# A fused attention and feed-forward block: first loads in chunks, put-off rotations, bank reads ahead of the maximum tree, and early row statistics

## The chip, the cores and the metric

The kernel runs on one core of a Trainium2 chip. The metric is the device time of one execution in microseconds. TensorE (PE) multiplies matrices and writes to PSUM banks; VectorE (DVE), ScalarE (ACT) and GpSimd (POOL) do the elementwise work; SyncE (SP) and ACT issue the transfers (DMA). Each engine works through its own list of instructions in order, and a semaphore holds an instruction back until what it needs is there.

## The reference

Two batches of 512 rows by 1024, all in fp32, and a context of 1024 rows by 1024 for each batch. `x` is the running row matrix:

```python
x = x + quantized_matmul(layernorm(x), ctx)             # both sides rounded to 0..255
x = x + ffn0(layernorm(x))                              # W.T, bias, LoRA mixed by a softmax router
h = layernorm(x)
q = rope(h @ wq)            # 32 heads of 128
k, v = rope(ctx @ wk), ctx @ wv                         # 8 heads, each for 4 query heads
x = x + softmax(q @ k.T / sqrt(128) + mask) @ v @ wo
x = x + ffn1(layernorm(x))                              # W_up.T, LoRA of the top-1 expert
```

## The kernel before

PE's order is written out by hand in the whole program. DVE, ACT and POOL follow the order of a scheduler, except in the attention, where the order of the code is taken as it stands. SP's list holds most transfers.

**Products in sevens.** Big products are done by a scheme with seven instead of eight products of quarter matrices. `left_sums` and `right_sums` make the four sums of quarters on each side. `seven` (for keys, values and queries) and `seven_onto` (for the output projection and the two feed-forward layers) run the products in a set order: 1, 2, 6, 7, 5, 4, 3 or 1, 6, 2, 7, 5, 4, 3. Product 2 is added in PSUM onto the bank of product 1, 4 onto that of 7, 3 onto that of 5; so before product 4 may start, someone must have read product 7 out of the bank they share. In `seven_onto` product 1 is copied out by ACT (L267), product 6 is added by DVE in L269, and all others by DVE in L272; POOL adds a further term in L274. The products of fp32 matrices appear in the trace as records of four to a product of 256 contraction rows and eight to one of 512.

**Banks.** PSUM has a pool "b" of four banks (products, attention results, the broadcast maxima) and a pool "wide" of two double banks (scores, transposes).

**The stages.** First come the keys and values of batch 0 in the order keys, values, keys, values (two quads each), with the quantized product of both batches woven in as `side` work; then batch 1, the first feed-forward layer (`linear`, `routed`), the queries in eight quads (`queries`), the attention, and the second feed-forward layer. Keys and queries are rotated by `rope`: two ACT operations of half the partitions (L192, L193), and three on DVE (L194, L197, L198); the result is then stored to DRAM from SP's queue.

**The attention loop** (`attention`) is a pipeline over 64 heads. A step `n` has three phases: the scores of head n+2 (L686, with the mask added on DVE in L700); then three or four products of the output projection of an earlier group (`stretches`) or, in the first steps, the last products of the last quad of queries (`extra["products"]`), alternating with the four operations of the maximum `tree` (L708, L710, L712, L714); then the third phase:

```python
            if old:
                old.turn_sum()
                old.attend(0)
            if mid:
                mid.place_maximum()
                mid.exponential(0)
```

`turn_sum` and `turn_maximum` transpose on PE (L650), reduce on DVE (L652) and store a row of 512 numbers to DRAM from ACT's queue (L659); `from_row` reads such a row back on all partitions, also from ACT's queue (L665). `place_maximum` copies the row of maxima to a bank (ACT, L728); `exponential` adds it (DVE, L732), takes the exponential (ACT, L735) and sums on POOL (L738 to L743). `attend` multiplies with the values (L749), and ACT copies the result out (L757). POOL normalizes in L760. A cycle of four steps holds 4, 3, 4 and 3 stretches.

**The tail.** When the last step with new scores is over, `normed` makes the normalized, transposed rows of batch 0 for the second feed-forward layer: for each of the four row tiles statistics (L163, L165), a root on ACT (L167), a reciprocal (L168), the scaling (L170) and eight transposes (L185), woven with the last steps of the attention. Then come the gate (L874) and `linear`.

Of the kernel before, what the change touches and what calls it, by code (L numbers as in the profile page):

```python
# [18 lines left out]
P = 128  # L19
# [20 lines left out]
def decoder_kernel(  # L40
# [119 lines left out]
    def layernorm(x_t):  # L160
        stats = small([P, 2, 6])
        for i in range(2):
            nc.vector.bn_stats(stats[:, i, :], x_t[:, ts(i, HALF)])  # L163
        mv = small([P, 2])
        nc.vector.bn_aggr(mv, stats)  # L165
        rstd = small([P, 1])
        nc.scalar.activation(rstd, mv[:, 1:2], AF.Sqrt, bias=eps_t)  # L167
        nc.vector.reciprocal(rstd, rstd)  # L168
        h = u4([P, D])
        nc.vector.tensor_scalar(h, x_t, mv[:, 0:1], rstd, ALU.subtract, ALU.mult)  # L170
        return h
# [32 lines left out]
    def left_sums(eng, a11, a12, a21, a22, fresh):  # L204

        s3, s2, s4 = fresh(), fresh(), fresh()
        eng.tensor_tensor(s3, a11, a21, ALU.subtract)
        eng.tensor_tensor(a21, a21, a22, ALU.add)
        eng.tensor_tensor(s2, a21, a11, ALU.subtract)
        eng.tensor_tensor(s4, a12, s2, ALU.subtract)  # L210
        return [a11, a12, s4, a22, a21, s2, s3]

    def right_sums(eng, b11, b12, b21, b22, fresh):

        t3, t2, t4 = fresh(), fresh(), fresh()
        eng.tensor_tensor(t3, b22, b12, ALU.subtract)
        eng.tensor_tensor(b12, b12, b11, ALU.subtract)
        eng.tensor_tensor(t2, b22, b12, ALU.subtract)
        eng.tensor_tensor(t4, b21, t2, ALU.subtract)
        return [b11, b21, b22, t4, b12, t2, t3]  # L220
# [193 lines left out]
    def keys(b, q, ctx_ops, w):  # L414
# [15 lines left out]
        return pair(group(0), group(1))  # L430

    def values(b, q, ctx_ops, w):
# [24 lines left out]
        return pair(blocks(0), blocks(1))  # L457

    def transposed_norm(b, places):

        h = None
        for t in range(NT + 1):
            ahead = layernorm(rows(b, t)) if t < NT else None
# [5 lines left out]
    def normed(b, tile, n):  # L469
# [4 lines left out]
        else:  # L474
# [3 lines left out]
            [[quarters[t // 2][j][:, :, ts(t % 2, P)] for t in range(NT)] for j in range(2)],  # L478
        )
# [116 lines left out]
    def queries(q, h_ops, w):  # L596
        def head(m):
# [7 lines left out]
            def emit(i, j, src):  # L605
                dst = u2([P, HALF]) if (i, j) == (0, 0) else src
                rope(dst, src, 0, ATT_SCALE)
                nc.sync.dma_start(q_d[j][4 * q + 2 * i + m], dst)

# [164 lines left out]
    def attention(extra):  # L774
# [23 lines left out]
        for n in range(-2, total + GRP + 1):  # L798
# [9 lines left out]
            if n == 2:  # L808
                w_ops = {i: output_operand(0, i) for i in (1, 6, 2, 7, 5, 4, 3)}
# [23 lines left out]
            for _ in range(3 + k % 2):  # L833
                next(tree, None)
                next(stretches, None)
# [3 lines left out]
            for _ in range(extra.pop(n, 0)):  # L839
                next(tree, None)  # L840
                next(extra["products"])
# [3 lines left out]

            if old:
                old.turn_sum()
                old.attend(0)
            if mid:
                mid.place_maximum()  # L850
# [9 lines left out]
            if old:  # L860
                old.attend(1)
            yield
# [51 lines left out]
    wk_raw, ctx_raw = [], [None] * 4  # L914
    for i, (wh, ch, kh) in enumerate((((0, 0), 0, 0), ((0, 1), 1, 0), ((1, 1), 0, 1), ((1, 0), 1, 1))):
        w = u4([P, 4, 256])
        (nc.sync if i % 2 else nc.scalar).dma_start(w, wk[0, wh[0], wh[1]])
        t = u8([P, 4, HALF])
        src = ctxT_in[0, ts(ch, 4 * P), ts(kh, HALF)].rearrange("(c p) n -> p c n", p=P)
        nc.scalar.dma_start(t[:, 0:2, :], src[:, 0:2, :])  # L920
        nc.sync.dma_start(t[:, 2:4, :], src[:, 2:4, :])
        wk_raw.append(w)
        ctx_raw[2 * ch + kh] = t
    wk_raw[2:] = wk_raw[3], wk_raw[2]
    late = u4([P, 2, HALF])
    nc.sync.dma_start(cos_t[0], cos_in[:, 0:HALF])
    nc.sync.dma_start(sin_t[0], sin_in[:, 0:HALF])
    nc.sync.dma_start(late[:, 0, :], cos_in[:, HALF:S2])
# [203 lines left out]
```

## Time and profile before

| | us |
|---|---|
| median of 4 runs | 2553.16 (2551.92 to 2556.35) |
| profiled execution | 2552.19 |
| its span | 2550.3 |
| PE busy | 2454.4 (96%) |
| DVE busy | 1867.0 (73%) |
| POOL busy | 1010.3 (40%) |
| ACT busy | 531.1 (21%) |
| DVE idle ahead of L732, behind ACT's L728 | 67.6 |
| DVE idle ahead of L272, behind PE | 126.5 |

The mean granted clock of PE is 0.991. In the page a group of instructions is given by line, engine, operation and tiles; "idle before, releaser" is the time in which that engine stood still just ahead of such an instruction, and what ended most of it. A busy PE is not PE at its peak: at the reduced clock the same matmul shows a longer time. The steady part of the attention runs from about 1141 to 2327 us, the tail with the last layer from there to 2550.

### The profile page before, as it was taken

The page shows a single profiled execution, that of the slowest core. Times are in us where ns is not written, and L with a number is a line of the kernel's source. Part 1 is how long each engine was busy: PE and PEld are TensorE (multiplying, and loading weights), DVE is VectorE, ACT ScalarE, POOL GpSimd, SP SyncE. Part 2 cuts the span into 40 slices and gives each one's busy share as a digit, 9 for nine tenths or more (in the row PEclk, how much of TensorE's full clock was granted, in tenths as well). Part 3 has the DMA queues.
Part 4 walks back from the last instruction along what each step waited for, and adds up shares of the span by engine and source line. Part 5 has one row for each costly group of instructions (what it writes and reads, how often), then busy time and mean ns, then how long its engine had stood idle before and what let it go on. Part 6 is the DMA issues. An engine that isn't in the chain of part 4 may idle for free.

```text
span 2550.3 us, 19683 instructions
## 1 busy us (share of the span) xinstructions
PE 2454.4 (96%) x6849; PEld 1213.9 (48%) x6856; DVE 1867.0 (73%) x2039; ACT 531.1 (21%) x618; POOL 1010.3 (40%) x536
## 2 busy tenths in 40 slices
PE   7999999999999998899999999999999999997999
PEld 3747567554444443344444444444444444443553
DVE  6778736447776557788888888888888888887542
ACT  1211112101222212222222222222222222223000
POOL 0000100210000002276767666766777676766221
PEclk9999999999999999999999999999999999999899
DMA  7334322024883312423322332443233323333200
GB/s 251 126 124 146 123 92 95 13 84 160 309 313 111 104 67 60 137 56 109 109 68 84 111 106 69 119 144 91 77 93 112 87 74 99 112 80 86 83 34 33
DMA packets 146946, 277.53 MB, mean 109 GB/s; under 512 B 29152, under 2 KB 46576, under 8 KB 145824
## 3 DMA queue, kind: packets, MB, share of 16 engines
q1 hardware_dynamic: 106064, 234.39, 27.7%
q10 hardware_dynamic: 40352, 41.17, 6.7%
q8 instruction: 55, 0.90, 0.2%
q0 software_dynamic: 432, 0.71, 0.1%
q14 instruction: 43, 0.35, 0.1%
HBM read 217.24 MB, written 58.98 MB: 108 GB/s over the span
## 4 chain that ended last, share of the span: by engine, by line
PE 45%; DVE 14%; issue 7%; ACT 1%; DMA 1%; POOL 0%; ACTq 0%; POOLq 0%; DVEq 0%; SPq 0%
PE b L299 18%; PE wide L686 14%; PE b L749 11%; DVE u L708 4%; DVE u L732 3%; DVE u L272 2%; PE wide L650 2%; DVE small L652 1%; DVE u L700 1%; DVE u L712 1%; PE b L874 1%; DVE u L714 1%; DMA row<-small 1%; ACT b L728 0%; DVE u L269 0%
## 5 line engine op out<-in xcount | busy, mean ns | idle before, releaser
L299 PE MATMUL b<-u,u 128*128 128x512 f32 (+1 forms) x3648 | 1421.8, 546 | 41.7 <-DVE u L272 16.8
L299 PEld LDWEIGHTS b<-u,u 128*128 128x128 f32 x3648 | 690.6, 191 | 736.2 <-issue 628.8
L686 PE MATMUL wide<-u,u 128*128 128x512 f32 x1024 | 463.1, 601 | 27.6 <-DVE small L652 13.8
L738 POOL TENSOR_TENSOR u<-u 128x1024 f32<-128x1024 f32 x64 | 151.5, 2366 | 797.5 <-ACT u L735 797.5
L749 PE MATMUL b<-u,u 128*128 128x512 f32 x1024 | 461.4, 594 | 0.0
L700 DVE TENSOR_TENSOR u<-wide,u 128x1024 f32<-128x1024 f32 x256 | 311.2, 1222 | 115.1 <-PE wide L686 115.0
L732 DVE TENSOR_TENSOR u<-u,b 128x2048 f32<-128x2048 f32 x128 | 292.1, 2282 | 67.6 <-ACT b L728 67.6
L686 PEld LDWEIGHTS wide<-u,u 128*128 128x128 f32 x1024 | 192.0, 191 | 287.9 <-issue 183.9
L735 ACT ACTIVATE u<-u 128x2048 f32<-128x2048 f32 x128 | 244.5, 1911 | 213.0 <-DVE u L732 196.0
L749 PEld LDWEIGHTS b<-u,u 128*128 128x128 f32 x1024 | 186.9, 192 | 185.1 <-issue 185.1
L274 POOL TENSOR_TENSOR u<-u,u 128x512 f32<-128x512 f32 x120 | 171.9, 1452 | 225.4 <-DVE u L272 205.3
L272 DVE TENSOR_TENSOR u<-u,b 128x512 f32<-128x512 f32 x200 | 135.5, 678 | 126.5 <-PE b L299 126.5
L741 POOL TENSOR_TENSOR u<-u,u 128x1024 f32<-128x1024 f32 x64 | 150.7, 2354 | 29.3 <-ACT u L735 28.3
L728 ACT COPY b<-u 128x512 f32<-128x512 f32 x64 | 37.7, 590 | 593.3 <-DVE small L723 436.7
L742 POOL TENSOR_TENSOR u<-u,u 128x1024 f32<-128x1024 f32 x64 | 151.5, 2367 | 4.9
L760 POOL TENSOR_TENSOR u<-u,u 128x512 f32<-128x512 f32 x64 | 139.1, 2173 | 13.9 <-DMA u<-row 13.9
L192 ACT ACTIVATE u<-u 64x512 f32<-64x512 f32 x72 | 45.2, 628 | 384.7 <-DVE u L245 222.7
L743 POOL TENSOR_TENSOR u<-u 128x512 f32<-128x512 f32 x64 | 121.2, 1894 | 4.9
L708 DVE TENSOR_TENSOR u<-u 128x1024 f32<-128x1024 f32 x64 | 116.6, 1822 | 8.4 <-PE wide L650 6.2
L710 DVE TENSOR_TENSOR u<-u,u 128x1024 f32<-128x1024 f32 x64 | 121.8, 1904 | 1.2
L650 PEld LDWEIGHTS wide<-ident,u 128*128 128x128 f32 x512 | 80.8, 203 | 66.8 <-issue 61.6
L951 POOL DMA_DIRECT2D u<-in_b_dram x1 | 0.6, 558 | 264.5 <-PE wide L400 264.5
(122 smaller groups left out, 1584.9 us busy)
## 6 DMA issues: line engine op xcount, KB each, us to landing
u<-row ACTq DMA_DIRECT2D x128, 256.0 KB, 3.6
u<-wo SPq DMA_DIRECT2D x64, 512.0 KB, 4.5
u<-in_wo_dram SPq DMA_DIRECT2D x48, 512.0 KB, 4.4
u<-in_wq_dram SPq DMA_DIRECT2D x32, 512.0 KB, 4.2
q<-u SPq DMA_DIRECT2D x64, 256.0 KB, 2.1
u<-in_wo_dram SPq DMA_DIRECT2D x16, 1024.0 KB, 7.4
wo<-u SPq DMA_DIRECT2D x32, 512.0 KB, 3.6
u<-q SPq DMA_DIRECT2D x64, 256.0 KB, 4.1
```

Of the source, the lines that this page charges most:

```text
L272: nc.vector.tensor_tensor(c, c, acc, ALU.add)
L274: nc.gpsimd.tensor_tensor(c, c, u, ALU.add)
L299: nc.tensor.matmul(acc, lhsT, rhs, start=start and k == 0, stop=k == len(pairs) - 1, skip_group_check=True,)
L686: nc.tensor.matmul(sc[:, ts(n, HALF)], self.kT[:, ts(2 * j + n, P)], self.qT, start=True, stop=True,)
L700: nc.vector.tensor_tensor(self.e[j // 2][:, js, :], sc.rearrange("p (k q) -> p k q", k=2), mask[j], ALU.add)
L708: nc.vector.tensor_tensor(m, e[0][:, 0:2, :], e[0][:, 2:4, :], ALU.max)
L732: nc.vector.tensor_tensor(e, e, self.nmf.unsqueeze(1).to_broadcast([P, 4, S]), ALU.add)
L735: nc.scalar.activation(e, e, AF.Exp)
L738: nc.gpsimd.tensor_tensor(d, e[:, 0:2, :], e[:, 2:4, :], ALU.add)
L741: nc.gpsimd.tensor_tensor(d, d, e[:, 0:2, :], ALU.add)
L742: nc.gpsimd.tensor_tensor(d, d, e[:, 2:4, :], ALU.add)
L749: nc.tensor.matmul(self.acc, self.v[:, k, :], self.e[j][:, k % 4, :], start=(k == 0), stop=(k == NKT - 1),)
```

## The change

Four things, in the order of the program.

1. The first loads. The first quarter of the weights and the first quarter of the context come in four chunks each, on two queues. The weights of both key quads of batch 0 are loaded ahead, the context of the second half of the rows after the first half. The products 1 and 2 of both groups of both key quads (eight products, 32 matmuls of 128 contraction rows each) run ahead of all sums. The sums are generators now, with another place for each result, and DVE's order is written out by hand for this part. The order of stages becomes keys, keys, values, values.
2. The last quad of queries puts its rotations (`rope` and the store) into a list, `later`, which is worked off at the end of phase 3 of each step. The products go 3, 2, 2, 2, 2, 2, 1 over seven steps, not 3, 3, 2, 2, 2, 2 over six. The first seven output operands are loaded at step 4, not 2.
3. In phase 2 `next(stretches)` stands ahead of `next(tree)`, so the read of a bank stands ahead of the tree operation on DVE; `next(extra["products"])` likewise. In phase 3 `place_maximum` stands first.
4. The row statistics of batch 0 for the last layer are made in the last four of the steps ahead of `normed`, one row tile a step, with one root for the four; `normed` then only scales.

```diff
+    def all_moments(b):
+
+        mv, ready = small([P, NT, 2]), []
+        for t in range(NT):
+            moments(rows(b, t), mv[:, t, :])
+            yield ready
+        rstd = small([P, NT])
+        nc.scalar.activation(rstd, mv[:, :, 1], AF.Sqrt, bias=eps_t)
+        nc.vector.reciprocal(rstd, rstd)
+        ready += [(mv[:, t, 0:1], rstd[:, t : t + 1]) for t in range(NT)]
+        yield ready
...
+    def left_steps(eng, a11, a12, a21, a22, fresh):
+
+        s1 = fresh()
+        eng.tensor_tensor(s1, a21, a22, ALU.add)
+        yield
+        s2 = fresh()
+        eng.tensor_tensor(s2, s1, a11, ALU.subtract)
+        yield
+        eng.tensor_tensor(a21, a11, a21, ALU.subtract)
+        yield
+        s4 = fresh()
         eng.tensor_tensor(s4, a12, s2, ALU.subtract)
-        return [a11, a12, s4, a22, a21, s2, s3]
-
-    def right_sums(eng, b11, b12, b21, b22, fresh):
-
-        t3, t2, t4 = fresh(), fresh(), fresh()
-        eng.tensor_tensor(t3, b22, b12, ALU.subtract)
-        eng.tensor_tensor(b12, b12, b11, ALU.subtract)
-        eng.tensor_tensor(t2, b22, b12, ALU.subtract)
+        yield [a11, a12, s4, a22, s1, s2, a21]
...
+    def right_steps(eng, b11, b12, b21, b22, fresh):
+
+        t1 = fresh()
+        eng.tensor_tensor(t1, b12, b11, ALU.subtract)
+        yield
+        t2 = fresh()
+        eng.tensor_tensor(t2, b22, t1, ALU.subtract)
+        yield
+        eng.tensor_tensor(b12, b22, b12, ALU.subtract)
+        yield
+        t4 = fresh()
         eng.tensor_tensor(t4, b21, t2, ALU.subtract)
-        return [b11, b21, b22, t4, b12, t2, t3]
+        yield [b11, b21, b22, t4, t1, t2, b12]
...
-    def queries(q, h_ops, w):
+    def queries(q, h_ops, w, later=None):
+
         def head(m):
             def product(i, acc, start):
                 accumulate(
@@ -602,10 +647,16 @@
                     start,
                 )
 
-            def emit(i, j, src):
+            def finish(i, j, src):
                 dst = u2([P, HALF]) if (i, j) == (0, 0) else src
                 rope(dst, src, 0, ATT_SCALE)
                 nc.sync.dma_start(q_d[j][4 * q + 2 * i + m], dst)
+
+            def emit(i, j, src):
+                if later is None:
+                    finish(i, j, src)
+                else:
+                    later.append(lambda: finish(i, j, src))
...
-            if n == 2:
-                w_ops = {i: output_operand(0, i) for i in (1, 6, 2, 7, 5, 4, 3)}
...
             for _ in range(3 + k % 2):
+                next(stretches, None)
                 next(tree, None)
-                next(stretches, None)
...
             for _ in range(extra.pop(n, 0)):
+                next(extra["products"])
                 next(tree, None)
-                next(extra["products"])
+            if n == GRP:
+                w_ops = {i: output_operand(0, i) for i in (1, 6, 2, 7, 5, 4, 3)}
...
+            if mid:
+                mid.place_maximum()
             if old:
                 old.turn_sum()
                 old.attend(0)
             if mid:
-                mid.place_maximum()
...
+            for act in extra["later"]:
+                act()
+            extra["later"].clear()
...
+    wk_raw = [[u4([P, 4, 256]) for _ in range(4)] for _ in range(2)]
+    ctx_raw = [u8([P, 4, HALF]) for _ in range(4)]
+
+    def load_weight(q, mh, ch):
+        nc.sync.dma_start(wk_raw[q][2 * mh + ch], wk[q, mh, ch])
+
+    def load_context(queue, ch, kh, cs):
+        queue.dma_start(
+            ctx_raw[2 * ch + kh][:, cs, :],
+            ctxT_in[0, ts(ch, 4 * P), ts(kh, HALF)].rearrange("(c p) n -> p c n", p=P)[:, cs, :],
+        )
+
+    for c in range(4):
+        cs = slice(c, c + 1)
+        nc.sync.dma_start(wk_raw[0][0][:, cs, :], wk[0, 0, 0][:, cs, :])
+        load_context(nc.scalar, 0, 0, cs)
+    load_weight(0, 0, 1)
+    load_context(nc.scalar, 1, 0, slice(0, 2))
+    load_context(nc.sync, 1, 0, slice(2, 4))
+    load_weight(1, 0, 0)
+    load_weight(1, 0, 1)
     nc.sync.dma_start(cos_t[0], cos_in[:, 0:HALF])
     nc.sync.dma_start(sin_t[0], sin_in[:, 0:HALF])
+    for ch in range(2):
+        load_weight(0, 1, ch)
+        load_context(nc.sync, ch, 1, slice(0, 4))
+    late = u4([P, 2, HALF])
     nc.sync.dma_start(late[:, 0, :], cos_in[:, HALF:S2])
     nc.sync.dma_start(late[:, 1, :], sin_in[:, HALF:S2])
     cos_t[1], sin_t[1] = late[:, 0, :], late[:, 1, :]
+    for ch in range(2):
+        load_weight(1, 1, ch)
+
+
+    ctx_ops = [ctx_raw[0], ctx_raw[2]] + [None] * 5
+    w = [wk_raw[q][0:2] + [None] * 5 for q in range(2)]
+    first = [keys(0, q, ctx_ops, w[q]) for q in range(2)]
+    with tc.manual_schedule(engines={mybir.EngineType.DVE}):
+        rights = right_steps(nc.vector, *ctx_raw, lambda: u8([P, 4, HALF]))
+        lefts = left_steps(nc.vector, *wk_raw[0], lambda: u4([P, 4, 256]))
+        advance(rights, 2)
+        advance(lefts, 2)
+        for g in first[0]:
+            next(g)
+        next(first[0][0])
+        next(rights)
+        next(lefts)
+        next(first[0][1])
+        w[0][:] = next(lefts)
+        ctx_ops[:] = next(rights)
+        for _ in range(2):
+            for g in first[1]:
+                next(g)
+    w[1][:] = quad_sums(wk_raw[1])
...
-        for i, stage in enumerate((keys, values, keys, values)):
-            main = stage(b, i // 2, ctx_ops, w)
-            weave(main, side, 2, 10 if b == 0 and i == 0 else 0)
-            if i < 3:
-                w = quad_weights((wk, wv)[(i + 1) % 2], (i + 1) // 2)
+            ctx_ops = context_sums(ctx_raw)
+        for i, stage in enumerate((keys, keys, values, values)):
+            if b == 0 and i < 2:
+                main = chain(*first[i])
+            else:
+                main = pair(*stage(b, i % 2, ctx_ops, w))
+            weave(main, side, 2, 6 if b == 0 and i == 0 else 0)
+            if i < 3 and (b, i) != (0, 0):
+                w = quad_weights((wk, wv)[(i + 1) // 2], (i + 1) % 2)
...
-    steps = attention({-2: 3, -1: 3, 0: 2, 1: 2, 2: 2, 3: 2, "products": main})
+    extra = {-2: 3, -1: 2, 0: 2, 1: 2, 2: 2, 3: 2, 4: 1}
+    steps = attention({**extra, "products": main, "later": later})
     with tc.manual_schedule(
         engines={
             mybir.EngineType.DVE,
@@ -1018,11 +1117,19 @@
             mybir.EngineType.Pool,
         }
     ):
-        for _ in range(3 * (B * NH + 2) - 6):
+        for _ in range(3 * (B * NH - 5)):
             next(steps)
-
-
-    hs, norms = normed(0, u4, 4)
+        stats = all_moments(0)
+        for _ in range(NT):
+            for _ in range(2):
+                next(steps)
+            ready = next(stats)
+            next(steps)
+        next(stats)
+        for _ in range(3):
+            next(steps)
+
+    hs, norms = normed(0, u4, 4, ready)
```

## The prediction

> **What bounds the kernel now.** I read the page first: TensorE (PE) is busy 2454.4 of 2550.3 us. That busy time also holds work at half clock, so the waits of PE and its timeline came next. First the waits of PE, whole run (total us, times, longest):
>
> ```profile
> PE b L299 <- DVE u L272: 16.8, 57, 1.3
> PE wide L185 <- DVE u L170: 13.9, 2, 9.7
> PE wide L686 <- DVE small L652: 13.8, 7, 2.9
> PE b L299 <- DMA u<-in_ctxT_in_dram: 13.1, 1, 13.1
> PE wide L686 <- DVE u L700: 11.9, 21, 1.3
> PE b L299 <- DVE u L218: 8.4, 2, 5.3
> ```
>
> These rows hold 78 of the 96 us in which PE idles, and the change touches each. Then PE's timeline (start, us, idle before in brackets), in the opening, a four-step cycle of the attention, and the tail:
>
> ```profile
> 13.07 15.93 PE L299 MATMUL b<-u,u 128*128 128x512 f32 x32 [13.07 <-DMA u<-in_ctxT_in_dram]
> 34.26 60.37 PE L299 MATMUL b<-u,u 128*128 128x512 f32 x192 [5.26 <-DVE u L218]
> ...
> 1222.50 1.99 PE L299 MATMUL b<-u,u 128*128 128x512 f32 x4 [0.28 <-DVE u L272]
> 1224.71 1.98 PE L299 MATMUL b<-u,u 128*128 128x512 f32 x4 [0.23 <-DVE u L272]
> ...
> 1258.12 3.70 PE L686 MATMUL wide<-u,u 128*128 128x512 f32 x8 [0.36 <-DVE u L700]
> ...
> 2336.79 1.94 PE L185 MATMUL wide<-ident,u 128*128 128x128 f32 x8 [9.65 <-DVE u L170]
> 2338.53 8.51 PE L299 MATMUL b<-u,u 128*128 128x512 f32 x16
> 2360.42 1.94 PE L185 MATMUL wide<-ident,u 128*128 128x128 f32 x8 [4.29 <-DVE u L170]
> ```
>
> Unit prices: a record of 512 columns has a pitch of 0.43 us, an eight-record product 3.44, a four-record stretch product 1.72. The first 32 records take 15.93 instead of 13.8, and 16 records after the 9.65 us gap take 8.51 instead of 6.87: a long gap costs 1.6 to 2 us of slow clock besides. Four records behind a short wait show 1.98 instead of 1.72, so each short stall costs its idle time and about 0.3 of refilling.
>
> On VectorE (DVE) and ScalarE (ACT) these rows matter; the first three are the DVE's in the step at 1214, the fourth in a step without GpSimd (POOL) work, the last three ACT's in the tail:
>
> ```profile
> 1219.96 1.88 DVE L708 TENSOR_TENSOR u<-u 128x1024 f32<-128x1024 f32 x1
> 1221.77 0.67 DVE L272 TENSOR_TENSOR u<-u,b 128x512 f32<-128x512 f32 x1
> 1230.43 2.29 DVE L732 TENSOR_TENSOR u<-u,b 128x2048 f32<-128x2048 f32 x1 [1.08 <-ACT b L728]
> 962.36 1.22 DVE L708 TENSOR_TENSOR u<-u 128x1024 f32<-128x1024 f32 x1
> 2356.58 0.56 ACT L757 COPY u<-b 128x512 f32<-128x512 f32 x1
> 2357.16 1.28 ACT L167 ACT_TABLE_LOAD   x1
> 2358.45 0.29 ACT L167 ACTIVATE small<-small,eps_t 128x1 f32<-128x1 f32 x1
> ```
>
> The evacuation L272, which frees a shared bank for PE, stands behind a tree operation of 1.88 us; and once per head the DVE waits 1.08 us for ACT's copy of the maxima (67.6 us in all on L732's page row).
>
> **A, the opening.** PE now starts at the first chunks. The first product needs 1.5 MB; by the transfer rates of the present opening (5.8 to 12.9 us for the first landings) I let it end at 11.4 (bounds 9 to 14), and seven more follow at 3.44: eight products done at 35.4. Today the eighth ends at 34.26 + 4 × 3.44 + 1.7 slow clock = 49.7, so the lead is 14.3. But all four banks "b" then hold first products, and DVE must free them. The second right sum needs the last context quarter, which lands around 27 (today all of it is in by 25.1; 0.5 MB more is now ahead of it; bounds 25 to 31). Behind it DVE has two left sums, two further right sums, the ropes (three operations of 0.61 each), the second quad's first sums and the row statistics, and some of these wait for x and context rows that the SP queue issues only after stores of kT. Laying the rows end to end, PE waits about 3.7 before the eleventh product and 6.4 before the twelfth, each with 1.6 of slow clock: 13.3 of the 14.3 are gone. From there DVE has a row of quantizations without a gap up to the fourth transposition, which comes out near 130; today's equal point is 116.7 + 4 × 3.44 = 130.5. Net gain **1** (bounds −6 to +8, mainly the landing of the last quarter, which passes through one to one). The order keys, keys, values, values changes no count; weight loads stay a stage ahead.
>
> **B, the start of the attention.** From 932.75 to 1140.9 PE loses 38.4 us against its pitches (13.8 of it on L652's rows: ropes of the last quad stand before the reduction that frees a wide bank). The eight ropes now go to the ends of the steps (1,1,1,2,0,2,1). L652's waits go. What is late next is the first score evacuation L700: the ropes stand ahead of it on DVE (1.8 us each), and their two rotations (0.63 each) on ACT behind the exponential (1.91), the row load's wait and the copy L757. In the step at 1234 these rows end near 1239.2, the rope at 1240.4 and L700 at 1241.6, and the third pair of scores, today at 1237.8, waits 3.8; about 1 less with C. So 1.6 to 3.3 for a step with one rope, about 5.1 with two, 8.1 at the first step with all phases: 25.6 in all, with some 7.5 of refill and slow clock 33. Net **5** (bounds −5 to +12). Each rope's store of q moves with it and holds SP's queue until the rope is done; behind it is the next head's q load, which is wanted a whole step later, so nothing. Cutting products to 3,2,2,2,2,2,1 moves work only. The first seven output operands are loaded two steps later, past the step's x loads on SP's queue; they are needed a step on, and land in 4.5 us each, cover enough; without it one landing, 4.5.
>
> **C, the steady attention.** A cycle of four steps takes 85.63; its PE work is 14 × 1.718 + 4 × (2 × 6.87 + 2 × 0.465) = 82.7. So 0.73 to 0.78 a step is lost, over 55 steps about 42: the five short stalls above with refill. With the bank read ahead of a tree operation, it is free 0.6 after its product's end, while PE still has another product of 1.72 in the other bank: L272's waits go. The copy L728 moves ahead of the sum's row store on ACT, so DVE starts L732 about a microsecond earlier and the L700 stall goes. What is late next: the tree's end. In the step at 1214 it comes out at 1228.9, when PE wants it at 1229.4; the second evacuation has 0.4 to spare. Half of the 55 steps have four stretches. If these slacks are gone, the two stalls of such a step (0.28 + 0.23 and twice 0.3, 1.1) come back, 27 × 1.1 = 30, and some 10 are left; if none is, 42. I let ten go, 27 × 0.37 (a hair of wait and the refill): **32** (10 to 42).
>
> The row for a tree operation is 1.22 where POOL is idle and 1.88 to 2.27 where POOL works; the change moves tree operations later, under POOL's normalization and additions. I keep today's contended rows, since POOL covers these operations already. The Trainium skill ("GPSIMD Engine Reference", Specifications) says that POOL's SBUF interface is shared with the DVE where a DVE instruction has two SBUF inputs, which is what tree operations are and evacuations are not: it speaks against this move, and by it, with every tree operation contended, the gain would be nearer the lower bound.
>
> **D, the tail.** The row statistics of batch 0 move into the last four steps. Today PE ends attending at 2327.1 and transposes at 2336.8, behind statistics, a root and a scaling. Now only the scaling (0.81) stands behind L732's end at 2329.1: start at 2330.0, 6.8 earlier, and 2.2 of slow clock saved. The 4.29 wait goes with its slow clock (0.9 and 1.8): 6.9. Together 15.9. Against it: four times 2 × 0.68 + 0.2 on DVE ahead of the sums' reduction, in steps with some 2 to 3 us of DVE idle time: 2 (0 to 6); the up-projection's weights now go last on SP's queue and their sums late on DVE: 2 (0 to 6); two more table loads of 1.28, one while ACT is idle, one under L732: 0.5. Net **11** (5 to 15). A table switch is told by "ScalarE: Activation LUTs" (What ACT_TABLE_LOAD costs) as 2.66 us with a drain; the rows above show 1.28 with no gap on either side, and by the page the term would be 1.4 to 2.8 worse.
>
> **Sum.** 1 + 5 + 32 + 11 = 49. The profiled execution took 2552.19 (span 2550.3), so 2503.2; the median of the runs shown is 0.97 higher, so 2504. Within the forecast the bounds add like independent errors: 7, 10, 22 and 6 make 26 the slow way, 7, 7, 10 and 4 make 15 the fast way: 2489 to 2530.
>
> **Rivals.**
> 1. *The opening gives all back and more.* If the last quarter lands at 31 and the x loads come behind the stores, A is −6 to −8: 2513. For it: a queue of 7.86 MB ahead, DMA at 390 to 410 GB/s already. Against: rates at 28 to 34 us show one queue alone holds 410.
> 2. *The put-off ropes cost more than the waits they remove*: two-rope steps of 7 with slow clock, B −10: 2519. For it: ACT's queue behind the exponential. Against: POOL and DVE have little else in those steps.
> 3. *Slower: the tree becomes the bound.* From one tree's end to the next there are 0.47 + 3.44 + 6.87, then with four stretches 1.72 + 4 × 0.6, with three 1.34 + 2 × 0.6, and the tree T: on average 14.1 + T against PE's 20.7. Today T is 1.88 + 1.69 + 1.69 + 1.16 = 6.4. At 7.3 C's gain is nothing (2536); at 7.6 the whole change is level; with three operations at L708's slowest row of that cycle, 2.27, T is 8.0, a step 22.1, 0.65 × 55 = 36 lost: 2552 + 36 − 17 = 2571.
> 4. *All waits named go and nothing takes their place*: 8 + 12 + 42 + 11: 2480.
> That the change doesn't do what it says is hardly open: in the changed order the evacuations do stand before the tree and the copy before the row store.
>
> **How the numbers follow.** Forecast 0.57; rival 1 0.10, 2 0.10, 3 at no gain in C 0.07 and beyond 0.08 (half of that near level), 4 0.08. The range 2482 to 2536 leaves out the far end of 3, and part of 4. Faster by over 0.2% (5 us, about what a measurement of this kernel can tell) 0.89, within 0.03, slower 0.08.
>
> **What would show it.** Right: L272's row in PE's waits nearly empty, L732's idle time far below 67.6, cycles near 83; PE's first matmul near 5 us, but new waits between 35 and 65; L652 rows replaced by L700 rows in the first seven steps; the first transposition of the tail 3 us after the last attend. Wrong: a wait of PE at L650 for L714 in every four-stretch step (rival 3), PE idle time over 20 us before 70 us (rival 1), or a start of the attention longer than 208 us at equal work (rival 2).

## The result and the profile after

The changed kernel takes 2554.77 us (median of 38 runs, 2551.99 to 2563.56), the kernel before 2552.60 beside it (59 runs): ratio 1.0008, 95% interval 1.0003 to 1.0013. I had 2504. The profiled execution took 2554.22, its span is 2552.4. Three marks that both kernels have split the two spans into stretches (us):

| stretch | before | after | difference | predicted |
|---|---|---|---|---|
| start to the first scores | 932.75 | 941.50 | +8.8 | A: −1 |
| first scores to the scores of step 6 | 192.68 | 224.60 | +31.9 | B: −5 |
| step 6 to step 58 | 1115.63 | 1079.98 | −35.7 | C: −32 |
| step 58 to the end | 309.24 | 306.32 | −2.9 | D: −11, and the last steps of C |

So the steady part came in as predicted, and the start of the attention and the opening ate it. The prediction's sum was 51 us off, and 37 of these lie in the second row. The waits of PE over the whole run, after (total us, times, longest; line 737 is the scores, 751 their reading by DVE, 340 the products, 284 the reading of product 7 in `seven`, 406 and 197 the transposition and the last step of quantized rows, 203 and 168 the transposes and the scaling of `normed`, 963 the copy of the transposed gate values):

```profile
PE wide L737 <- DVE u L751: 57.5, 11, 11.6
PE b L340 <- DMA u<-in_ctxT_in_dram: 9.4, 4, 4.3
PE b L340 <- DVE u L284: 8.9, 2, 5.6
PE wide L406 <- DVE u L197: 6.0, 3, 4.6
PE wide L203 <- DVE u L168: 2.9, 1, 2.9
PE b L340 <- DVE u L963: 2.9, 1, 2.9
```

The 57 waits on L272 (16.8 us) are down to 0.4 us (L313), those on the reductions from 13.8 to 1.4, the transposes from 13.9 to 2.9; in their place stands one row of 57.5 us, eleven waits of up to 11.6. The other stall that part 3 was to remove, DVE's idle time ahead of the addition of the maxima, is gone too (67.6 us before, now nothing), as the page's row shows, after:

```profile
L783 DVE TENSOR_TENSOR u<-u,b 128x2048 f32<-128x2048 f32 x128 | 290.2, 2267 | 0.0
```

PE's timeline shows where the waits are. Rows from the opening, two steps at the start of the attention, two steady steps and the last step with scores, after ("..." stands for rows left out):

```profile
4.02 2.08 PE L340 MATMUL b<-u,u 128*128 128x512 f32 x2 [4.02 <-DMA u<-in_ctxT_in_dram]
...
14.55 37.27 PE L340 MATMUL b<-u,u 128*128 128x512 f32 x82 [4.31 <-DMA u<-in_ctxT_in_dram]
57.44 50.89 PE L340 MATMUL b<-u,u 128*128 128x512 f32 x112 [5.62 <-DVE u L284]
...
135.66 1.04 PE L406 MATMUL wide<-ident_b,u 128*128 128x128 bf16 x8 [4.64 <-DVE u L197]
...
996.85 5.89 PE L737 MATMUL wide<-u,u 128*128 128x512 f32 x8 [9.07 <-DVE u L751]
...
1118.61 6.44 PE L737 MATMUL wide<-u,u 128*128 128x512 f32 x8 [11.65 <-DVE u L751]
...
1249.26 7.03 PE L737 MATMUL wide<-u,u 128*128 128x512 f32 x16
...
1270.81 7.03 PE L737 MATMUL wide<-u,u 128*128 128x512 f32 x16
...
1290.63 7.03 PE L737 MATMUL wide<-u,u 128*128 128x512 f32 x16
...
2320.05 6.47 PE L737 MATMUL wide<-u,u 128*128 128x512 f32 x8 [4.88 <-DVE u L751]
```

Two steps with seven stretches take 1290.63 − 1249.26 = 41.37 us, 20.7 a step, with no wait: PE's own work. At the start there are six long waits: 4.80, 9.07, 6.64, 9.63, 11.65 and 8.08 us. Each is followed by eight records in 5.5 to 6.4 us where 3.6 is the rule, so every gap also costs 1.9 to 2.8 us of slow clock. Behind the longest the granted clock is 0.50 from 1118.6 to 1124.0; from 940 to 1170 us it is 0.88 on average, and before it was 0.97 in that stretch. DVE between two scores of such a step, after:

```profile
1100.74 2.28 DVE L783 TENSOR_TENSOR u<-u,b 128x2048 f32<-128x2048 f32 x1
1106.76 1.25 DVE L212 SCALAR_TENSOR_TENSOR u<-u,cos_t 128x512 f32<-128x512 f32 x1 [3.74 <-ACT u L211]
1107.93 2.82 DVE L215 TENSOR_TENSOR u<-u,sin_t 128x512 f32<-128x512 f32 x1
1110.79 1.64 DVE L216 TENSOR_TENSOR u<-u,u 128x512 f32<-128x512 f32 x1
1112.34 1.74 DVE L212 SCALAR_TENSOR_TENSOR u<-u,cos_t 128x512 f32<-128x512 f32 x1
1114.01 1.74 DVE L215 TENSOR_TENSOR u<-u,sin_t 128x512 f32<-128x512 f32 x1
1115.79 1.63 DVE L216 TENSOR_TENSOR u<-u,u 128x512 f32<-128x512 f32 x1
1117.34 2.34 DVE L751 TENSOR_TENSOR u<-wide,u 128x1024 f32<-128x1024 f32 x2
```

DVE waits 3.74 for ACT's second rotation (L211); but then two ropes take 10.6 us, not 2 × 1.8, and only then are the scores read, whose two banks PE wants back. POOL's rows at that time show what makes them long, after (L793 and L794 are sums of the exponentials, L811 the normalization):

```profile
1107.54 2.67 POOL L793 TENSOR_TENSOR u<-u,u 128x1024 f32<-128x1024 f32 x1
1110.28 1.59 POOL L794 TENSOR_TENSOR u<-u 128x512 f32<-128x512 f32 x1
1111.83 1.71 POOL L811 TENSOR_TENSOR u<-u,u 128x512 f32<-128x512 f32 x1
```

POOL's operation of 1107.54 ends at 1110.21, and DVE's of 1107.93 at 1110.75; the next two pairs end at 1111.87 and 1112.43, and at 1113.54 and 1114.08. Seventeen operations of the put-off ropes with both inputs in SBUF start while a POOL operation runs, and each of them ends 0.55 us after it. So in these rows DVE does not run slower beside POOL; it stands until POOL's running operation is over.

### The profile page after: what moved, and what is told of

The parts are those of the page before. It is cut to its first block, busy times and chain, and to the rows that moved or that the text cites. A ratio compares the mean times of both kernels' runs of the same rounds, so it can differ in the third digit from the quotient of the medians.

```text
span 2552.4 us, 19686 instructions
## 1 busy us (share of the span) xinstructions
PE 2452.8 (96%) x6848; PEld 1225.3 (48%) x6856; DVE 1856.6 (73%) x2036; ACT 528.4 (21%) x615; POOL 996.7 (39%) x536
## 5 line engine op out<-in xcount | busy, mean ns | idle before, releaser
L737 PE MATMUL wide<-u,u 128*128 128x512 f32 x1024 | 469.6, 611 | 59.5 <-DVE u L751 57.5
L737 PEld LDWEIGHTS wide<-u,u 128*128 128x128 f32 x1024 | 199.3, 196 | 318.4 <-issue 187.9
L315 POOL TENSOR_TENSOR u<-u,u 128x512 f32<-128x512 f32 x120 | 186.8, 1576 | 223.0 <-DVE u L313 208.4
L313 DVE TENSOR_TENSOR u<-u,b 128x512 f32<-128x512 f32 x200 | 135.8, 680 | 135.3 <-PE b L340 135.2
L793 POOL TENSOR_TENSOR u<-u,u 128x1024 f32<-128x1024 f32 x64 | 152.8, 2388 | 5.0
L811 POOL TENSOR_TENSOR u<-u,u 128x512 f32<-128x512 f32 x64 | 113.1, 1767 | 14.9 <-DMA u<-row 14.9
L759 DVE TENSOR_TENSOR u<-u 128x1024 f32<-128x1024 f32 x64 | 109.1, 1705 | 0.0
L761 DVE TENSOR_TENSOR u<-u,u 128x1024 f32<-128x1024 f32 x64 | 102.4, 1600 | 0.2
L794 POOL TENSOR_TENSOR u<-u 128x512 f32<-128x512 f32 x64 | 97.7, 1527 | 4.9
L703 DVE TENSOR_REDUCE small<-wide 128x4 f32<-128x512 f32 x128 | 87.2, 682 | 8.0 <-PE wide L701 8.0
```

The source lines that it names most:

```text
L313: nc.vector.tensor_tensor(c, c, acc, ALU.add)
L315: nc.gpsimd.tensor_tensor(c, c, u, ALU.add)
L737: nc.tensor.matmul(sc[:, ts(n, HALF)], self.kT[:, ts(2 * j + n, P)], self.qT, start=True, stop=True,)
L793: nc.gpsimd.tensor_tensor(d, d, e[:, 2:4, :], ALU.add)
L811: nc.gpsimd.tensor_tensor(self.oT, self.oT, self.den, ALU.mult)
```

## The experiments

"Router" below is the start of PE's matmuls for the second router product, a mark at which all kernels have done the same work since the start: 505.2 us before, 519.65 after. It judges the opening by itself. These marks and stretches come from one profiled execution of each kernel: the five kernels that have the opening of the changed one (after, no_b, no_d, b_no_pool, b_after_scores) show the router at 517.4 to 520.0. "Start" is the stretch from the first scores to those of step 6.

**Each part undone, and part 3 alone.** Theory: the losses lie where the table has them and each part stands by itself. Rival, in the expectations: the parts interact.

```diff
# no_b
-            else queries(q, h_ops, w, later if q == NH // 4 - 1 else None)
+            else queries(q, h_ops, w, None)
-    extra = {-2: 3, -1: 2, 0: 2, 1: 2, 2: 2, 3: 2, 4: 1}
+    extra = {-2: 3, -1: 3, 0: 2, 1: 2, 2: 2, 3: 2}
# no_a: opening, stage order, left_sums and right_sums of the kernel before
# no_d: range(3 * (B * NH + 2) - 6), normed(0, u4, 4) of the kernel before
# c_alone: the kernel before with
             for _ in range(3 + k % 2):
-                next(tree, None)
                 next(stretches, None)
+                next(tree, None)
...
             for _ in range(extra.pop(n, 0)):
-                next(tree, None)
                 next(extra["products"])
+                next(tree, None)
...
+            if mid:
+                mid.place_maximum()
             if old:
                 old.turn_sum()
                 old.attend(0)
             if mid:
-                mid.place_maximum()
                 mid.exponential(0)
```

> The changed kernel with the put-off rotations undone: each rope is issued behind its product again, and the products go 3, 3, 2, 2, 2, 2 over six steps. From the first scores to the scores of step 6 the changed kernel took 31.9 us longer than the kernel before (224.6 against 192.7). Theory 1, each part costs by itself what its stretch shows: all of that comes back and the order of part 3 helps a little, 2519 to 2524 us, the stretch at 186 to 193 us. Rival, the loss is an interaction with part 3 (products ahead of the tree, the copy of the maxima first), with the ropes only where it shows: less than half comes back, 2538 to 2555 us, the stretch at 208 us or more.

Measured: 2510.28 us, ratio to before 0.9840 (0.9825 to 0.9854); start 184.0. The whole loss came back and 12 us more than the table had, some 44 in all, more than theory 1 expected. The profile has 40.6 of it in the start; 2.3 come ahead of the router, where the edit changes nothing.

> The changed kernel with the opening, the order of stages and the sums of the kernel before. The changed kernel reaches its first scores 8.75 us later than the kernel before. Theory 1: these 8.75 come back, 2545 to 2548 us, first scores near 932.7. Rival, the opening itself gains and its loss is given by the tails of later stages whatever the opening: first scores no earlier than 938, time 2552 or more.

Measured: 2543.37, ratio 0.9965 (0.9953 to 0.9977); first scores at 930.8, router at 505.0. About 11 came back, somewhat more than theory 1 had; in the profile 10.7 by the first scores and 5.5 in the tail, less some 2 in the steps between. So part 1 costs in the tail too.

> The changed kernel with the row statistics of batch 0 where the kernel before has them. From the scores of step 58 to the end the changed kernel took 3.0 us less than the kernel before. Theory 1: the time rises by about 3, 2556 to 2559 us; the wait of 4.88 us at the third scores of the last step goes, those of 9.65 and 4.29 at the transposes come back. Rival, the statistics cost more in the last four steps than they bring: time falls to 2550 or less.

Measured: 2553.43, ratio 1.0009 (0.9999 to 1.0018); from step 58 to the end 303.5. Part 4 brought nothing in the changed kernel; neither theory's time was met.

> The kernel before with part 3 alone: bank reads ahead of tree operations, the copy of the maxima first in the third phase. Theory 1: 52 steps at 20.77 instead of 21.45 us, 36 us less, 2515 to 2519 us, the start of the attention as before or some us shorter. Rival, the faster steady state needs the other parts too: gain under 20, 2533 or more.

Measured: 2503.80, ratio 0.9812 (0.9795 to 0.9828): 48 us less, 12 more than expected. The steady stretch is 1081.3, 34.3 less. The start falls from 192.7 to 188.6 and the tail from 309.2 to 300.2. In the tail one wait of 10.01 is left at the transposes, the other (4.29, with its half clock) has gone. So part 3 took a good part of what I had booked under D. Its two moves, the bank reads and the copy of the maxima, were not run apart.

**What makes the put-off rotations dear.** Theory 1: the place, ahead of the score additions; and POOL's sums, which make the rows long. Rival: ACT's wait, or that DVE has no room anywhere.

```diff
# b_no_pool, in exponential(), for the first seven heads
+            if self.hd + NH * self.b < 7:
+                if j == 0:
+                    self.d = u4([P, 2, S])
+                else:
+                    nc.gpsimd.memset(self.d[:, 0, :], 1.0)
+                return
# b_after_scores: the loop over extra["later"] moves
-            for act in extra["later"]:      # end of phase 3
+            for act in extra["later"]:      # after the scores, at the head of phase 2
```

> The changed kernel without POOL's sums of the exponentials for the first seven heads: their denominators are left at one. In the changed kernel a rope operation on DVE takes up to 2.82 us where 0.68 was counted, while POOL adds. Theory 1, POOL's additions make these operations slow and thereby two to three us of each wait: the rope rows are at 0.68, the waits of PE at the third scores fall from 4.8 to 11.7 us to 4 to 8, the stretch from the first scores to step 6 from 224.6 to 205 to 212 us. Rival, the wait is ACT's alone (exponential, copy, rotations): rope rows fall but the stretch stays above 218.

This kernel leaves out the sums of seven denominators and serves as a probe alone. Measured in one run: start 206.6, 18 less than 224.6. The first rope of a step with two, without POOL's sums:

```profile
1044.27 0.69 DVE L212 SCALAR_TENSOR_TENSOR u<-u,cos_t 128x512 f32<-128x512 f32 x1 [3.74 <-ACT u L211]
1044.88 0.69 DVE L215 TENSOR_TENSOR u<-u,sin_t 128x512 f32<-128x512 f32 x1
1045.60 0.69 DVE L216 TENSOR_TENSOR u<-u,u 128x512 f32<-128x512 f32 x1
```

The wait for ACT is the same 3.74; the rows here are back at 0.69. PE's six long waits fall from 49.9 to 34.0 us in all, and with about 2 us less of slow clock behind them that is the whole 18. In the other step with two ropes POOL sums the output operands at that time; four of the six rope rows take 1.64 to 1.75 there, and PE still waits 9.08. So POOL's sums of the exponentials are 18 us of the loss, and POOL's other work some more.

> The changed kernel with the put-off rotations issued after the scores of the next step, at the start of phase 2, not ahead of them. Theory 1, the place ahead of the score additions is what costs (PE has two wide banks and waits for the first to be read): the waits at the third scores go, the tree comes out later instead, the stretch from the first scores to step 6 falls from 224.6 to 186 to 198 us, time 2516 to 2530. Rival, any place in the step costs as much, since DVE and ACT have no room: the stretch stays above 212.

Measured: 2509.23 in one run, start 176.9, below the range expected and better than with the rotations undone (184.0). The time is that of no_b (2510.28) all the same, since the first scores come 6 us later in this run. The waits of PE that are left there (line 701 transposes for the maxima, 765 ends the tree), in this kernel:

```profile
PE wide L701 <- DVE u L765: 11.6, 4, 7.8
PE wide L737 <- DVE u L751: 10.6, 7, 5.7
```

The waits at the scores fall from 57.5 to 10.6 us, of which 5.7 stand at the last step with scores and belong to part 4; the tree comes out later instead, in four steps. The place was the fault, not the putting off.

**Part 4 with one line moved; the new sums by themselves.** Both on top of part 3 alone.

```diff
# c_d_late
         nc.scalar.activation(rstd, mv[:, :, 1], AF.Sqrt, bias=eps_t)
+        yield ready
         nc.vector.reciprocal(rstd, rstd)
...
         next(stats)
         for _ in range(3):
             next(steps)
+        next(stats)
# c_sums: left_steps and right_steps in place of the old sums, nothing else of part 1
```

> Part 3 on the kernel before, and part 4 with one line moved: the reciprocal of the root stands after the last step with scores, not before it. In the changed kernel DVE waits 4.12 us at that reciprocal for ACT's root, and PE 4.88 us behind it, at half clock afterwards. Theory 1, part 4 is sound and lost its gain at this one instruction and to part 3, which had taken the second wait of the tail already: the tail from step 58 to the end, 300.2 us with part 3 alone, falls to 290 to 294; time 2493 to 2498 against 2503.8 of part 3 alone. Rival, the statistics themselves press on DVE in the last steps: the tail stays at 298 or more, 2502 or more.

Measured: 2499.87, ratio 0.9787 (0.9761 to 0.9813); tail 294.3, 6 us less than with part 3 alone. Just outside the expectation, but for its reason: in PE's waits the last step with scores shows 0.61 instead of 4.88, the transposes 3.39 instead of 10.01. The intervals of the two ratios overlap, so the 6 us rest on the profiles.

> Part 3 on the kernel before, with the sums in the places and the order of the changed kernel and nothing else of part 1. Theory 1: the changed tails and the faster stretch between 505 and 932 us come from these sums, since the scheduler orders DVE by them: the wait for the transposed gate values (2.86 us) appears in the tail, the tail grows by 3 to 5 us, and the stretch from the second router product to the first scores shrinks by 4 to 6; time within 3 us of 2503.8. Rival, both come from the order of the stages and the loads: neither stretch moves by more than 1 us.

Measured: 2497.80, ratio 0.9783 (0.9763 to 0.9803). The wait for the gate values came (2.87), as expected; the stretch from router to first scores did not shrink in this run (428.1, before 427.5). The tail grew by 2.5, a little less than expected. What I had not expected: the router comes 5.2 us earlier, at 500.0. The old sums had the third before the second; the new give the two that product 6 needs first, and PE's 5.26 at 34 us turns into waits of less than 1.

**The opening, part by part.** best1 joins part 3, the new sums, part 4 with the line moved and the rotations after the scores; the others change the opening only.

```diff
# best_order, on best1
-        for i, stage in enumerate((keys, values, keys, values)):
+        for i, stage in enumerate((keys, keys, values, values)):
# best_chunks, on best1: first weight and context quarter in four chunks
+            for c in range(4):
+                nc.sync.dma_start(w[:, cs, :], wk[0, 0, 0][:, cs, :])
+                nc.scalar.dma_start(t[:, cs, :], src[:, cs, :])
# the next four: the changed kernel with the rotations after the scores, and
# late_side: weave(main, side, 2, 16 ...) for 6
# early4: without "for g in first[1]: next(g)" twice
# no_hand: without manual_schedule(engines={DVE}) in the opening
# rows_pool: rows of x and context of batch 0 by nc.gpsimd.dma_start
```

> The opening and the stage order of the kernel before with the new sums, part 3, part 4 with the reciprocal moved behind the last scores, and the put-off rotations issued after the scores. Theory 1, these parts add: 2497.8 of part 3 with the new sums, less 9 to 12 at the start of the attention (188 to 177), less 4 to 6 in the tail: 2480 to 2486 us. Rival, they share what they gain (the tail and the start are bound by DVE, whatever the order): 2490 or more.

Measured: 2485.75, ratio 0.9744 (0.9729 to 0.9758); start 177.7, router 500.0. The time is that of theory 1, but in part by luck: the start gave its 12 us, the tail only 1.9 (300.9 against 302.8), and 4.6 came between router and first scores, where best1 changes nothing.

> The kernel best1 with only the order of stages of part 1: keys, keys, values, values. The second router product starts at 505.2 us in the kernel before, at 500.0 with the new sums alone, at 519.65 in the changed kernel. Theory 1, the order of stages costs most of these 20 us, since two key stages in a row put sixteen ropes on DVE while it quantizes: router product at 512 to 518. Rival, the cost comes from the early products that hold four banks and the loads, not the order: router product at 498 to 503.

Measured: 2484.84, ratio 0.9741 (0.9726 to 0.9755); router 501.5. The rival held: the order of stages costs 1.4 at the router at most, and nothing that the times show.

> The kernel best1 with only the chunked loads of the first two quarters of part 1: products start at the first chunk, the rest of the opening as in best1. Theory 1, PE starts at 4 to 5 us, but the products behind the first four wait for the right sums, which wait for the last context quarter at 25 to 29 us: the router product moves by less than 3 us (498 to 502). Rival, the earlier start carries through: router product at 490 to 495.

Measured: 2482.43, ratio 0.9736 (0.9718 to 0.9755); router 500.3. PE starts at 4.02, and waits 3.19 for the sums at 29.90: an early start by itself carries nothing through.

> The changed kernel with the put-off rotations after the scores, and with the quantized product woven in from the 17th product of the first stages on, not the 7th. Its opening is otherwise that of the changed kernel, with the router product at 517.7 to 519.7. Theory 1, quantization rows between the evacuations on DVE make PE wait 5.6 us before the twelfth product and 4.6 at the fourth transposition: both waits go and the router product comes at 505 to 512. Rival, the rows only move and the waits with them: router product at 516 or later.

This kernel and the next three were run once each, for the router mark. Measured: router 530.1, 12 later than without the edit: the wait at 57 us stays (6.07), and later ones of 5.9 and 5.8 come at 241 and 261. The rival's side, and beyond it: the quantization was rather too late than too early.

> The opening of the changed kernel with only the four products of the first key quad ahead of the sums, not eight; rotations put off to behind the scores. The router product stands at 517.7 us with eight. Theory 1, the eight products hold all four banks and put their ropes and both quads' sums on DVE in a row, ahead of evacuations and quantization: with four, the wait before the twelfth product and that at the fourth transposition go, router product at 499 to 506. Rival, the loads and the order written by hand cost it: router product at 512 or later.

Measured: router 508.0, 9.7 earlier; both waits are gone, and one of 6.18 stands at 33.9 us instead. Just outside the range of theory 1.

> The opening of the changed kernel with eight early products, but DVE's order there left to the scheduler; rotations put off to behind the scores. Theory 1, the eight products are the cause whatever DVE's order: router product at 513 to 522, near the 517.7 with the order by hand. Rival, the order by hand is the cause: 498 to 507.

Measured: router 513.4, 4.3 earlier: on the lower edge of theory 1. The wait at the twelfth product is 1.08, that at the fourth transposition still 4.64.

> The opening of the changed kernel with the rows of x and of the context of batch 0 loaded from POOL's queue, not SP's, where they stand behind stores of kT; rotations put off to behind the scores. Theory 1, as predicted, the wait before the twelfth product is DVE waiting for a context row: that wait (5.6 us) falls below 2 and the router product moves from 517.7 to 508 to 514. Rival, DVE's order alone decides: it stays at 515 or later.

Measured: router 523.1, later by 5.4. The rows came early, beside the first loads (POOL's queue moved 4.91 MB between 20 and 70 us), and the right sums came later (the one that needs the last context quarter starts at 36.0 instead of 28.9). The wait at the twelfth product fell to 2.72, but one of 5.09 stands one product ahead of it. So my reading of that wait is not borne out as a gain, and the test disturbed what it was to hold still.

**The sums in the tail.**

```diff
# best2, on best_chunks: the sums of the last layer in the old order
+    w_ops = matrix(wupT, u8, 4, right_old)
+    ... token_sums(hs, lambda: u4([P, 4, 256]), left_old)
```

> The kernel best_chunks with the old order of the sums in the last layer only (the weights of the up-projection and its tokens). With the new order PE waits 2.87 us there for the transposed gate values, which DVE copies behind three sums of 2.2 us. Theory 1, that wait is the whole price of the new sums in the tail: it goes, about 1 us at the last gate transpose comes back as in the kernel before, and the time is 1 to 3 us below best_chunks, 2479 to 2482 us. Rival, the tail is bound elsewhere: no change, 2482 to 2484.

> The kernel best_chunks again, beside best2 on one chip: 2482 us, ratio 0.973 to 0.974 to the kernel before.

Measured side by side: best2 2476.69, ratio 0.9713 (0.9699 to 0.9726); best_chunks 2481.40, ratio 0.9721 (0.9708 to 0.9735). The intervals overlap, so the ratios alone do not tell them apart; in the profiles the wait of 2.86 is gone, and from the first gate's transposes to the end best2 takes 149.6 us, best_chunks 152.7. So some 3 us belong to the edit, the upper end of what was expected, and the rest of the 4.7 to the runs. best2 has the lowest time here, 2.9% below the kernel before.

## Why the prediction was wrong

Most of its signs of being right came: L272's row emptied, L732's idle time went, PE's first matmul stood at 4.02 us, two steady steps took 41.37, the first transposes of the tail came 2.92 after the last attend. None of them tested B. The sign that did, a start longer than 208 us, came as well (224.6). It was named under rival 2, which pointed the right way and took a third of the loss. A time within 0.2% of the kernel before had got a chance of 0.03.

**C, right.** The size was 32, the trace has 35.7 for 52 steps. The rival in which the tree becomes the bound didn't come about: the four tree operations, 1.71, 1.60, 1.44 and 0.90 on average (L759, L761, L763, L765), add up to 5.6 us, where the kernel before has 6.2 (L708, L710, L712, L714) and 7.3 decides. The contention of POOL and DVE, which I had put down against this move, cost nothing here: it lengthens tree operations in both kernels, and not more after than before. That part 3 also speeds the first steps, by 4 us, and the tail, by 9, was missing from the sum: I had booked the tail's second wait under D.

**B, the failed step.** Undone, it gives some 44 us; I had it at a gain of 5, and its losses at 25.6 of waits and 7.5 of clock. The mechanism was in the text (score additions behind the ropes, ropes behind ACT). The terms were mis-sized: the six long waits are 49.9 us and the slow clock behind them 14.3, together 64 where the sum had 33.

What failed first is the price of a rope, put at 1.8 us of DVE. Of the eight ropes, six took 4.4 to 5.6 us; one took 3.0, with POOL done half-way, and the first took 1.9, with POOL idle. Without POOL's sums of the exponentials 18 us come back (b_no_pool). The Trainium skill ("GPSIMD Engine Reference", Specifications) has exactly this, contention where a DVE instruction has two SBUF inputs, and the trace agrees: with the accumulator in PSUM the first rope operation takes 0.69 under POOL's work, from SBUF 1.24 to 1.74. I applied the rule to the tree and not to the operations that the change moves. The rest of the 44 is the place itself, ahead of the score additions and behind ACT: with the ropes behind the scores the start takes 176.9 us, POOL's sums included (b_after_scores). Last, the half clock: I took 7.5 us over the whole start for refill and clock, and each of the six waits is followed by 1.9 to 2.8 us of it. Rival 2 gave as evidence against itself that POOL and DVE have little else to do there; that was wrong.

**A, the failed step.** Up to the twelfth product the sum came out, in part by luck. Laid end to end its terms start that product at 57.4 us, and it starts at 57.44, after a wait of 5.62. On the way the fourth chunk came at 14.55, beyond the bounds (product 1 was to end by 14 at the latest), and the wait of 3.7 before the eleventh product did not come; the last context quarter let DVE go at 28.9 (taken 27). The rate of 410 GB/s that is read there for 28 to 34 us holds to about 30 in the trace; from 31 to 34 next to nothing moves.

What failed is the row of quantizations "without a gap up to the fourth transposition, which comes out near 130": that transposition came at 135.66, after a wait of 4.64, and waits of 1.1, 1.0 and 3.3 followed at 245 to 340, none of which was a term. Up to the router product the changed kernel is 14.4 behind: 6.4 in PE's waits (25.6 against 19.2), and the other 8 in longer rows of matmuls; the clock is granted at 0.50 from 11.4 to 18.2, 55.8 to 62.6, 134.3 to 141.1 and 339.1 to 342.5. With the ropes after the scores the same opening has the router at 517.7, 17.4 behind that of best_chunks (500.3). Of these the runs put 9.7 on the eight early products instead of four (early4), 4.3 on DVE's order by hand (no_hand), 1.4 on the order of stages, each from single profiles; some 2 are left over if these add, which was not shown. Why the quantization is late with eight products was argued from DVE's rows, in which it stands behind readings of products that PE does later; moving it later or loading its rows earlier made it worse, and so this stays open. From the router to the first scores the changed kernel is 5.7 us faster. The four kernels with the old sums take 425.8 to 427.7 there, those with the new ones 421.8 to 424.3 but for two at 427.4 and 428.1: likely the sums, not settled.

**D, the failed step.** 11 became nothing. The stretch from step 58 to the end is 309.2 us before, 300.2 with part 3 alone, 300.8 with parts 2 to 4 (no_a) and 306.3 with all four: so in these profiles part 4 cost 0.6 on top of part 3 (2.8 by no_d), and part 1, for which the sum had no term here, cost 5.5 (its sums by themselves 2.5, c_sums), 2.9 of them at the wait for the gate values. One of the two waits that D was to remove had gone with part 3. And a wait took its place that the sum did not have: the reciprocal of the four roots waits on DVE for ACT's root, ahead of the score readings of the last step. DVE, after:

```profile
2312.31 2.28 DVE L783 TENSOR_TENSOR u<-u,b 128x2048 f32<-128x2048 f32 x1
2318.70 0.18 DVE L187 RECIPROCAL small<-small 128x4 f32<-128x4 f32 x1 [4.12 <-ACT small L186]
```

and ACT ahead of it, after:

```profile
2316.50 0.57 ACT L808 COPY u<-b 128x512 f32<-128x512 f32 x1
2317.08 1.28 ACT L186 ACT_TABLE_LOAD   x1
2318.38 0.30 ACT L186 ACTIVATE small<-small,eps_t 128x4 f32<-128x4 f32 x1
```

The root stands behind ACT's copy of the attention result, so DVE stands 4.12 and PE 4.88, with eight records in 6.47 instead of 3.6 after it. Moved behind the last scores, part 4 brings 6 us on top of part 3 with the old sums (c_d_late). The table load is 1.28 with no gap on either side here too; the 2.66 of "ScalarE: Activation LUTs" (What ACT_TABLE_LOAD costs) does not show.

## What to carry to other kernels

Work that is put off to a quiet place is not quiet if the next reader of a scarce buffer stands behind it: ask, for each moved instruction, which engine's list it now heads, whose buffer is read next there, and what the other engines do at that moment (each moved DVE operation with two SBUF inputs stood until POOL's running addition was over). Moving the read of a shared bank ahead of longer work that nobody waits for yet, together with an earlier copy of the maxima, cost nothing and gave nearly 2% here. And a change of several parts is to be run in parts: one of the four was worth 48 us, and the other three together hid it.

## What was unexpected of the hardware

A DVE operation of 128 by 512 with both inputs in SBUF took 1.2 to 2.8 us when it started while a POOL operation ran, and 0.69 otherwise; with one input in PSUM it took 0.69 in either case. Its end follows POOL's: 0.55 us after the end of the POOL operation that was running, in all 17 such operations of the put-off ropes, and 1.08 to 1.15 us after it in all 138 tree operations of 128 by 1024 that started under one. A wait of PE of 4.8 to 11.7 us in the attention of the changed kernel was each time followed by 1.9 to 2.9 us of slow clock, so that a gap of five us cost seven to eight; one of 1.4 or 1.5 us was followed by 0.1.
